# A graph attention kernel in which SyncE fetches, one by one, a part of the node rows that GpSimd gathered

## The chip, the cores and the metric

The kernel runs on one core of one Trainium2 chip. The metric is the device time of one execution, in microseconds (us). The kernel before takes 4064.29 us, the median of three runs (4062.84 to 4064.88). An engine is named as in the profile: PE (TensorE, matrix products), DVE (VectorE, elementwise work), ACT (ScalarE), POOL (GpSimd) and SP (SyncE, which here only issues transfers). A queue that carries a q, as SPq, is the engine's own issuing of transfers.

## The reference

A graph has 6250 nodes of 256 numbers and 200000 edges, sorted by destination; every edge has 32 numbers of its own. The nodes pass a layer norm and two graph attention layers (four heads, then one). What matters of a layer, with the self loops and the edge gate left out:

```python
hx = (x @ Wg).reshape(n, h, f)
al = leaky_relu(dot(hx, a_s)[src] + dot(hx, a_d)[dst] + dot(he, a_e), 0.2)
m = segment_max(al, dst)
al = exp(al - m[dst])
al = al / segment_sum(al, dst)[dst]
out = segment_sum(hx[src] * al[:, :, None], dst) + b
```

So for every edge the row of its source node is fetched (`hx[src]`), weighted, and summed over the edges of one destination. The sources are in no order: the fetch is a gather of 200000 rows, in each of two layers.

## The kernel before

The 200000 edges are cut into 1563 chunks of 128, and these into 66 superchunks of 24 chunks (the last two are shorter). A node table in DRAM, `T[0]` or `T[1]`, holds for each node its 256 transformed numbers and a few logit terms, 268 or 260 numbers of four bytes that an edge needs. `steps` lists the 66 superchunks of the first layer and then the 66 of the second; the loop in `edges` makes one of them per pass, and prepares the next one (`nx`) in the same pass.

The parts of a pass, in the order of the code:

- `nodes` (L936, L938): SP loads the rows of 112 destination nodes of the superchunk two ahead into `tw`. The row number is a register that SP loads first from `base_i` (L927). Each of four `tw` buffers comes free when `finish` of the superchunk four back has read it.
- `load_lb`, `load_ea`, `load_fl` (L896, L921): SP loads the position rows `lb` (384 KB) and the edge numbers `ea` (768 KB) of two superchunks together, every second pass, and flags `fl` every fourth.
- `gather(nx)` (L871): POOL issues 24 indirect transfers, one per chunk, the last chunk first. Each fetches 128 rows of the table into one column of `G`. There are three buffers of `G`.
- `logits(st)` (L1071 and on), `ends`, `links`, `maxima`: DVE makes the logits and the running maxima, with small transposes on PE. This needs all 24 columns of `G`.
- `spread`, `parts`, `rphase1`, `rphase2`, `adst`: the edge part of `nx`. `parts` reads `tw` on DVE (L1021, for two superchunks at a time in every second pass), PE multiplies `ea` (L968), ACT takes the result (L969), PE collects it in `zad`.
- `scale(st)` (L1180): DVE multiplies all 24 columns of `G` by the weights. `carried` adds the sums brought over from the superchunk before.
- `sums(st)` (L1192): PE sums the rows by destination, 24 products with a one-hot matrix `S`.
- `rows3` (L1326 in the first layer, L1331 in the second): SP stores finished node rows.
- `edge_rows(nx)` (L1057, L1060): DVE turns `zad` into rows `rt` and sums them to `ade`, which `logits` of the next pass reads.
- `onehots(nx)` (L1008): DVE makes `S` of the next superchunk.
- `finish(pv)` (L1208 to L1279): DVE and ACT close the superchunk before. `evict(st)` (L1197): ACT takes the sums out of PSUM. `rows1`: PE and ACT turn the closed rows.

Every engine works through its own instructions in the order of the code and waits by semaphores for what it reads or overwrites. Nothing reorders them. The transfers that SP issues take turns on eight completion semaphores (DMAHW0 to DMAHW7): before SP issues one, the transfer eight back must have landed. The last three superchunks of a layer have their own code (`ending`).

Of the kernel before, what the change touches and what calls it, by code (L numbers as in the profile page):

```python
# [22 lines left out]
F32 = mybir.dt.float32  # L23
BF = mybir.dt.bfloat16
I32 = mybir.dt.int32
AF = mybir.ActivationFunctionType
# [5 lines left out]
P = 128  # L32
C = 24
# [13 lines left out]
def cuts(E):  # L47

    n = -(-E // P)
    k = -(-n // C)  # L50
    if k == 1:
        return [n]
    rest = n - C * (k - 2)
    return [C] * (k - 2) + [rest - rest // 2, rest // 2]


class Layer:

    def __init__(self, l):
        self.l = l
        self.H = H = HEADS[l]
        self.F = D // H
        self.p = D
        self.g = D + H
        self.one = D + H + 1
        self.gr = self.ad = D + H + 2
        self.m = self.ln = D + 2 * H + 2
        self.W = D + 3 * H + 2  # L70
        self.MW = D + 2 * H + 2
        self.TW = self.MW + (2 if l == 0 else 0)
# [7 lines left out]
class Kernel:  # L80
    def __init__(self, nc, tc, a, N, E, ctx):
        self.nc, self.tc, self.a, self.N, self.E, self.ctx = nc, tc, a, N, E, ctx
        self.cs = cuts(E)
        self.NS = len(self.cs)
        self.NCH = sum(self.cs)
        self.L = [Layer(0), Layer(1)]

    def pool(self, name, bufs=1, ctx=None, **kw):
# [548 lines left out]
    def edges(self, ctx):  # L637
        nc = self.nc
        self.gp += [self.pool(f"gath{i}", 1, ctx) for i in range(1, 3)]
        self.sp = self.pool("onehot", 2, ctx)  # L640
        self.wp = self.pool("work", 2, ctx)
        self.np_ = self.pool("nodes", 2, ctx)
        self.xp = self.pool("index", 1, ctx)
        self.ps_y = self.pool("ps_y", 1, ctx, space=PSUM)
        self.ps_1 = self.pool("ps_1", 1, ctx, space=PSUM)
        self.ps_f = self.pool("ps_f", 1, ctx, space=PSUM)
        self.lf = self.ps_1.tile([P, 512], F32, name="lf")
        nc.vector.memset(self.lf[0:4, 0:1], -BIG)
        steps = self.steps
        self.state = {0: None, 1: None}  # L650
        self.nodes(steps[0])
        self.gather(steps[0])
        if self.NS % 2:
            self.load_lb(1)
        self.spread(steps[0])
        self.parts(steps[0])
        self.blocks(steps[0])
        drain(self.rphase1(steps[0]))
        self.load_ea(1)
        self.rphase2(steps[0])  # L660
        self.adst(steps[0])
        self.onehots(steps[0])
        drain(self.soon)
        self.edge_rows(steps[0])

        pv = late = None
        self.ahead, self.rest = 1, None
        for k, st in enumerate(steps):
            nx = steps[k + 1] if k + 1 < len(steps) else None
            if st["s"] + 2 >= self.NS:  # L670
                continue
            for q in steps[k + 1:k + 3]:
                if q["L"] is st["L"] and "tw" not in q:
                    self.nodes(q)
            self.load_lb(k + 2)
            left = 99
            if self.ahead < len(self.groups):
                left = self.groups[self.ahead][0] - 2 - (self.ahead + 2 >= len(self.groups)) - k
            if self.rest is None and left <= 2:
                gi = self.index_load(self.ahead, self.xp)  # L680
                self.rest = self.index_group(self.ahead, self.xp, gi)
            if st["s"] + 3 == self.NS:
                self.ending(st, *steps[k + 1:k + 3], pv, late, steps[k + 3] if k + 3 < len(steps) else None)
                pv = late = None
                continue
            self.gather(nx)
            drain(self.logits(st))
            self.ends(st)
            self.spread(nx)
            self.parts(nx)  # L690
            y = self.rphase1(nx)
            next(y)
            self.links(st)
            if late:
                self.rows2(late)
            self.load_fl(k + 1)
            self.blocks(nx)
            drain(self.maxima(st))
            drain(y)
            self.load_ea(k + 2)  # L700
            self.rphase2(nx)
            self.adst(nx)
            if "S" not in st:
                self.onehots(st)
            drain(self.scale(st))
            self.carried(st)
            self.sums(st)
            if late:
                self.rows3(late)
                late = None  # L710
            self.edge_rows(nx)
            self.onehots(nx)
            if pv:
                drain(self.finish(pv))
            self.evict(st)
            if pv:
                self.rows1(pv)
                late = pv
            self.index_on(left)
            if st["s"] + 4 == self.NS:  # L720
                drain(self.finish(st))
            if k >= 6:
                next(self.late, None)
                next(self.late, None)
            pv = st
        self.flag()

# [126 lines left out]
    def flag(self):  # L854
# [6 lines left out]
        nc.vector.tensor_reduce(f[:, 0:1], ps[0:1, 0:n], axis=AX.X, op=OP.add)  # L861
        nc.vector.tensor_scalar(self.flag_i, f[:, 0:1], 0.0, None, op0=OP.is_equal)

    def gather(self, st):
        nc, L = self.nc, st["L"]
        st["G"] = G = self.G0 if st["k"] == 0 else self.gp[st["k"] % 3].tile([P, C, 270], F32, name="G")
        n = self.N
        idx = self.src[:, st["o"]:st["o"] + st["C"]]
        last = st["C"] - 1
        for c in (range(0) if st["k"] == 0 and self.CX > last else (last, *range(last))):  # L870
            nc.gpsimd.indirect_dma_start(  # L871
                out=G[:, c, 0:L.TW], out_offset=None, in_=self.rows[L.l][0:n * (1 + L.l), :],
                in_offset=bass.IndirectOffsetOnAxis(ap=idx[:, c:c + 1], axis=0))
# [582 lines left out]
def drain(g):  # L1456
    for _ in g:
        pass
# [22 lines left out]
def layout(inputs):  # L1481
# [3 lines left out]
    cs = cuts(E)  # L1485
    NS, NCH = len(cs), sum(cs)
    a = {"x": np.concatenate([x, np.zeros((2 * P, D), np.float32)])}
# [7 lines left out]
    nx = np.full(EP, END_DST, np.int32)  # L1495
# [3 lines left out]
    srcp, dstp, dnxp = (np.empty((P, NCH), np.int32) for _ in range(3))  # L1499
# [5 lines left out]
    for s, c in enumerate(cs):  # L1505
        e0, e1 = o * P, (o + c) * P
        nx[e1 - 1] = END_DST
        for t, v in ((srcp, sp), (dstp, dp), (dnxp, nx)):
# [11 lines left out]
        o += c  # L1520
    a.update(gsrc=sp.reshape(-1, 1), gdst=gdst.reshape(-1, 1), gdrow=gdst,
             gea=np.ascontiguousarray(eap.T))
    a.update(src=srcp, dst=dstp, dnx=dnxp, drow=drow, prow=prow, sdst=sdst,
             dpv=np.ascontiguousarray(prow[:, 3].T),
             srow=np.ascontiguousarray(sp[:cs[0] * P].reshape(P, -1).T),
# [26 lines left out]
```

## Time and profile before

| what | value |
|---|---|
| median of three runs | 4064.29 us |
| the profiled execution's own time | 4068.59 us |
| its span (first to last instruction) | 4066.2 us |
| busy: POOL, DVE, PE, ACT | 3012.7, 2855.0, 2696.3, 519.9 us |
| indirect transfers of L871 | 3102, 2959.9 us busy, 954 ns each |
| granted clock of TensorE | 0.789 |

The profile counts an engine as busy while it runs an instruction of its own; issuing a transfer counts as busy on POOL, where the engine makes the descriptors, but not on SP. A row of the groups has the line, engine and operation, what is written and read, the count, the busy time with the mean of one, and the idle time before them with what ended most of it. A row of the waits has the waiting engine, line and tile, what ended the wait, and then us in total, times, longest. A row of the timeline has the start and duration in us.

### The profile page before, as it was taken

How to read it: one execution, taken by the hardware profiler on the slowest of the kernel's cores; microseconds unless marked ns; L12 is line 12 of the kernel's file. 1: busy time of each engine (PE TensorE's matmuls, PEld its weight loads, DVE VectorE, ACT ScalarE, POOL GpSimd, SP SyncE). 2: the span in 40 equal slices, each digit the busy share in tenths (PEclk: the TensorE clock that was granted, in tenths of full speed). 3: DMA queues.
4: the chain of work that ended last, by engine and by line, in shares of the span. 5: the costliest groups of instructions: out<-in, count | busy, mean ns of one | idle time of the engine just before them, and what ended most of it. 6: DMA issues, size and time to landing. Idle time of an engine off the chain costs nothing.

```text
span 4066.2 us, 34155 instructions
## 1 busy us (share of the span) xinstructions
PE 2696.3 (66%) x9878; PEld 1737.4 (43%) x9878; DVE 2855.0 (70%) x6188; ACT 519.9 (13%) x1158; POOL 3012.7 (74%) x3255
## 2 busy tenths in 40 slices
PE   8776666666666766766646656666657666666665
PEld 6454444444444444444433433433434334334334
DVE  7887877877877877777856656656566566565666
ACT  5211111111111111111110000000000000000000
POOL 5777777777777777777747777777777777777775
PEclk9888888887887788888777787777777777777777
DMA  7455555555555555555434455455455445445443
GB/s 251 137 152 140 146 149 140 145 149 144 142 150 147 140 148 147 141 147 148 134 103 133 136 142 141 130 141 140 132 140 140 134 137 143 132 137 142 132 137 96
DMA packets 231085, 576.17 MB, mean 142 GB/s; under 512 B 63097, under 2 KB 87871, under 8 KB 230825
## 3 DMA queue, kind: packets, MB, share of 16 engines
q0 software_dynamic: 150144, 422.75, 39.6%
q1 hardware_dynamic: 80331, 150.52, 11.4%
q8 instruction: 79, 1.29, 0.1%
q14 instruction: 115, 0.94, 0.1%
q10 hardware_dynamic: 416, 0.67, 0.1%
HBM read 542.72 MB, written 31.09 MB: 141 GB/s over the span
## 4 chain that ended last, share of the span: by engine, by line
POOL 53%; issue 19%; DVE 19%; DMA 4%; PE 4%; ACT 1%; SPq 0%; DVEq 0%; ACTq 0%; POOLq 0%
POOL G L871 53%; DVE G L1180 6%; DMA G<-T,src 4%; DVE S L1008 3%; DVE lb L992 1%; PE ps L444 1%; PE y L968 1%; PE u L1192 1%; DVE rt L1057 1%; DVE m L1131 1%; DVE ade L1060 0%; DVE G L1169 0%; DVE fb L1126 0%; DVE al L1075 0%; DVE al L1073 0%
## 5 line engine op out<-in xcount | busy, mean ns | idle before, releaser
L871 POOL DMA_INDIRECT G<-T,src x3102 | 2959.9, 954 | 1001.1 <-issue 929.7
L1192 PE MATMUL u<-G,S 128*128 128x270 f32 (+1 forms) x6252 | 1617.9, 423 | 250.8 <-DVE G L1170 247.2
L1192 PEld LDWEIGHTS u<-G,S 128*128 128x128 f32 x6252 | 1295.4, 209 | 585.6 <-DVE G L1170 314.7
L1180 DVE TENSOR_TENSOR G<-G,kps 128x6144 f32<-128x6144 f32 (+2 forms) x140 | 853.3, 6099 | 0.0
L1071 DVE TENSOR_TENSOR G<-rt,G 128x96 f32<-128x96 f32 (+1 forms) x132 | 30.3, 229 | 910.3 <-DMA G<-T,src 910.0
L1099 PE MATMUL lf<-ident,fb 128*36 128x128 f32 (+1 forms) x132 | 49.5, 375 | 710.8 <-DVE fb L1088 684.3
L1008 DVE TENSOR_TENSOR S<-kps,loc 128x3072 f32<-128x3072 f32 x132 | 437.5, 3315 | 4.6
L968 PE MATMUL y<-ea,webd 64*128 64x256 f32 (+1 forms) x1056 | 396.7, 846 | 51.4 <-ACT R L969 51.4
L977 PE MATMUL zad<-R,wea 128*64 128x384 f32 (+1 forms) x1056 | 301.2, 711 | 158.4 <-ACT R L969 158.1
L969 ACT ACTIVATE R<-y,webd 128x1024 f32<-128x1024 f32 (+2 forms) x264 | 235.6, 892 | 1226.0 <-PE y L968 741.5
L1099 PEld LDWEIGHTS lf<-ident,fb 128*36 128x36 f32 (+1 forms) x132 | 15.6, 118 | 752.5 <-DVE fb L1088 725.2
L977 PEld LDWEIGHTS zad<-R,wea 128*64 128x64 f32 x1056 | 86.7, 185 | 426.0 <-ACT R L969 340.6
L968 PEld LDWEIGHTS y<-ea,webd 64*128 64x128 f32 x1056 | 125.6, 291 | 125.5 <-ACT R L969 70.4
L1197 ACT ACTIVATE U<-u 128x270 f32<-128x270 f32 (+1 forms) x132 | 51.9, 394 | 645.9 <-PE u L1192 645.9
L1029 PE MATMUL zad<-a,Q 128*128 128x12 bf16 (+1 forms) x132 | 26.1, 198 | 160.1 <-DVE a L1024 160.1
L444 PE MATMUL fin<-wg,h1T 128*128 128x260 f32 x264 | 128.7, 638 | 3.7 <-ACT h1T L1287 3.7
L1057 DVE STREAM_TRANSPOSE rt<-zad 128x768 f32<-128x768 f32 (+1 forms) x130 | 124.5, 957 | 5.1 <-PE zad L1043 5.1
L992 DVE TENSOR_TENSOR lb<-lb,kps 128x1536 bf16<-128x1536 bf16 (+1 forms) x68 | 113.5, 1670 | 0.0
L1222 ACT ACTIVATE mw<-mw,mg 128x2 f32<-128x2 f32 x66 | 19.7, 298 | 623.9 <-DVE mg L1221 623.9
L1029 PEld LDWEIGHTS <-Q 128*128 128x128 bf16 x132 | 16.0, 121 | 172.7 <-DVE a L1024 165.8
L1043 PE MATMUL zad<-lb,aq 128*128 128x384 bf16 (+1 forms) x264 | 86.5, 421 | 0.0
L444 PE MATMUL ps<-wg,hT 128*128 128x266 f32 x292 | 83.2, 410 | 1.7 <-ACT hT L326 1.6
(190 smaller groups left out, 2109.8 us busy)
## 6 DMA issues: line engine op xcount, KB each, us to landing
G<-T,src POOLq DMA_INDIRECT x3102, 2.8
ea<-in_ea_dram SPq DMA_DIRECT2D x64, 768.0 KB
lb<-locrow SPq DMA_DIRECT2D x64, 384.0 KB
T<-t1row SPq DMA_DIRECT2D x66, 227.5 KB
tw<-T SPq DMA_DIRECT2D x66, 225.8 KB
tw<-T SPq DMA_DIRECT2D x66, 117.2 KB
tw<-in_x_dram SPq DMA_DIRECT2D x66, 112.0 KB
out_dram<-fb SPq DMA_DIRECT2D x64, 112.0 KB
```

What stands on the lines that cost most here:

```text
L444: self.nc.tensor.matmul(ps[:, :L.MW], hT[:, k, :], self.wg[L.l][:, k, :], start=(k == 0), stop=(k == 1))
L871: nc.gpsimd.indirect_dma_start(out=G[:, c, 0:L.TW], out_offset=None, in_=self.rows[L.l][0:n * (1 + L.l), :], in_offset=bass.IndirectOffset ...
L968: nc.tensor.matmul(y[:, i, :n], self.webd[l][r, :], ea[r, w], start=True, stop=True)
L969: nc.scalar.activation(R[:, :, w], y[:, :, :n], AF.Relu, bias=self.be[l])
L977: nc.tensor.matmul(st["zad"][i * PH:(i + 1) * PH, o], self.wea[l][0], R[:, i, w], start=True, stop=False)
L992: V.tensor_tensor(lb[:, :, :n], lb[:, :, :n], self.k_part.unsqueeze(2).to_broadcast([P, i, n]), op=OP.is_equal)
L1008: nc.vector.tensor_tensor(st["S"][:, c0:c1, :], self.k_iota.unsqueeze(1).to_broadcast(w), self.loc[:, o + c0:o + c1].unsqueeze(2).to_broad ...
L1043: self.nc.tensor.matmul(st["zad"][:, o], st["aq"].rearrange("p k j -> p (k j)"), st["lb"][:, w], start=False, stop=True)
L1057: V.transpose(rv[:, :32 * c].rearrange("p (b n) -> p b n", b=2), z.rearrange("p (b n) -> p b n", b=2)[:, :, :16 * c])
L1099: self.nc.tensor.transpose(self.lf[0:e.shape[1], 1:P + 1], e, self.ident)
L1180: nc.vector.tensor_tensor(v, v, pw[:, c0:c1, :].unsqueeze(3) .to_broadcast([P, c1 - c0, H, L.F]), op=OP.mult)
L1192: nc.tensor.matmul(st["u"][:, :L.W], S[:, i, :], G[:, i, 0:L.W], start=(j == 0), stop=(j == c - 1))
```

## The change

`sides` names every third superchunk of a layer, 3, 6, 9 and so on to 60: 20 in each layer. For these POOL leaves out the gather of the last chunk. Its 128 rows are fetched by SP instead, each with a transfer of its own. A list of the 128 source numbers is loaded into a row `si`; eight loads bring 16 of them each into SP's registers; each register gives the place of one row in the table, and the row goes to one partition of a buffer `side`, of which there is one. `side` is a generator that hands out one transfer at a time, and `pump` draws 14, 15 and 14 of them at three places in a pass, over the three passes before the superchunk is worked on (43 x 3 = 129, the list and 128 rows). `placed(nx)`, at the end of the third pass, has ACT copy `side` into the last column of `G`.

In every pass `edge_rows(nx)` moves from its place ahead of `onehots(nx)` to the end of the pass, and in one pass of each layer the additional `finish(st)` comes after it.

The core of the diff:

```diff
+def sides(cs):
+    return [s for s in range(3, len(cs) - 3, 3)]
@@ edges
+        self.fp = self.pool("rows", 1, ctx)
+        self.flow = iter(())
         for k, st in enumerate(steps):
             nx = steps[k + 1] if k + 1 < len(steps) else None
+            if k + 3 < len(steps) and st["L"] is steps[k + 3]["L"] and steps[k + 3]["s"] in self.sides:
+                self.flow = self.side(steps[k + 3])
             if st["s"] + 2 >= self.NS:
                 continue
+            self.pump(14)
             for q in steps[k + 1:k + 3]:
                 if q["L"] is st["L"] and "tw" not in q:
                     self.nodes(q)
@@
                 self.rows2(late)
+            self.pump(15)
             self.load_fl(k + 1)
@@
             self.load_ea(k + 2)
+            self.pump(14)
             self.rphase2(nx)
@@
-            self.edge_rows(nx)
             self.onehots(nx)
@@
-            if st["s"] + 4 == self.NS:
-                drain(self.finish(st))
             if k >= 6:
                 next(self.late, None)
                 next(self.late, None)
+            self.placed(nx)
+            self.edge_rows(nx)
+            if st["s"] + 4 == self.NS:
+                drain(self.finish(st))
@@
+    def pump(self, n):
+        for _ in range(n):
+            if next(self.flow, self) is self:
+                break
+
+    def side(self, st):
+        nc, L, j = self.nc, st["L"], self.sides.index(st["s"])
+        idx = self.fp.tile([1, P], I32, name="si")
+        nc.sync.dma_start(idx, self.a["side"][j:j + 1, :])
+        st["row"] = R = self.fp.tile([P, self.L[0].TW], F32, name="side")[:, 0:L.TW]
+        yield
+        for b in range(0, P, 16):
+            _, rows = nc.values_load_multi_w_load_instructions(
+                idx[0:1, b:b + 16], engines=(mybir.EngineType.SP,), min_val=0, max_val=self.N - 1,
+                skip_runtime_bounds_check_because="sources are nodes")
+            for i, r in enumerate(rows):
+                nc.sync.dma_start(R[b + i:b + i + 1, :], self.T[L.l][ds(r, 1), 0:L.TW])
+                yield
+
+    def placed(self, st):
+        if "row" in st:
+            drain(self.flow)
+            L = st["L"]
+            self.nc.scalar.activation(st["G"][:, st["C"] - 1, 0:L.TW], st["row"], AF.Copy)
@@ gather
         for c in (range(0) if st["k"] == 0 and self.CX > last else (last, *range(last))):
+            if c == last and "row" in st:
+                continue
             nc.gpsimd.indirect_dma_start(
@@ layout
+    last = [sum(cs[:s + 1]) - 1 for s in sides(cs)] or [0]
+    a.update(side=np.ascontiguousarray(srcp[:, last].T))
```

How the rows of SP stand now is seen in the first layer, at a place where one side buffer is full and the next begins. Before, SP's rows from one store of finished node rows (`T_61<-t1row`) to the next were these, where `tw_175` is the buffer of destination rows, ISA the register arithmetic of the transfer behind it, and TENSOR_LOAD the load of a register:

```order
L1326 DMA T_61<-t1row_171 112x520
L927 TENSOR_LOAD base_i
L936 ISA
L936 DMA tw_175<-T_60 112x268
L938 ISA
L938 DMA tw_175<-in_x_dram 112x256
L921 DMA fl<-flags 4x516 x2
L1326 ISA
L1326 DMA T_61<-t1row_173 112x520
```

In the changed kernel the last row of one side buffer, the store, and the first rows of the next side buffer follow each other:

```order
L895 DMA side<-T_60 1x268
L1369 ISA
L1369 DMA T_61<-t1row_171 112x520
L887 DMA si<-in_side_dram 1x128
L891 TENSOR_LOAD si
L895 ISA
L895 DMA side<-T_60 1x268
```

Thirteen rows of `side` now stand between that store and the load of `tw_175`, which followed the store directly.

On DVE, in the first layer, `edge_rows` (`rt`, `ade`) stood before the one-hot matrix `S` and the closing of the superchunk before (`cnt`, then more):

```order
L448 TENSOR_TENSOR t1row_173<-fin,bias_373 128x260
L1057 STREAM_TRANSPOSE rt<-zad 128x768
L1060 TENSOR_REDUCE ade<-rt 128x96
L1005 COPY kps<-lastloc 128x1
L1008 TENSOR_TENSOR S<-kps,loc 128x3072
L1208 TENSOR_SCALAR cnt<-U 128x1
```

In the changed kernel they stand behind the last rows of that closing and directly ahead of the next superchunk's logits (`G<-rt,G`):

```order
L1312 TENSOR_TENSOR fb<-fa,fb 128x256
L1320 TENSOR_TENSOR t1row_171<-tw_175,hw 128x256
L1322 TENSOR_TENSOR t1row_171<-t1row_171,fb 128x256
L1100 STREAM_TRANSPOSE rt<-zad 128x768
L1103 TENSOR_REDUCE ade<-rt 128x96
L1114 TENSOR_TENSOR G<-rt,G 128x24x4
```

The two rows moved past `S` and the closing of a superchunk; nothing else on DVE moved.

1 line of the change is left out of this document (added).

## The prediction

> **What bounds the kernel now.** I read the page first, then the waits in total and by layer, POOL's gathers by stretch, and SP's timeline over two passes. The waits of the whole run (us in total, times, longest):
>
> ```profile
> POOL G L871 <- issue: 929.7, 3050, 0.3
> DVE G L1071 <- DMA G<-T,src: 910.0, 123, 20.4
> POOL G L871 <- DMA T<-t1row: 40.5, 1, 40.5
> ```
>
> 3050 of POOL's 3102 gathers waited for nothing but the 0.3 us that lies between any two of them; DVE waited 910 us for gathers. The gathers alone, in a stretch of each layer (length, busy time and count):
>
> ```profile
> 200.00:1940.00 1740.00, 1319.61 (x1379) 0.83 0.53 146
> 2150.00:3980.00 1830.00, 1386.06 (x1457) 0.75 0.50 138
> ```
>
> 1740 / 1379 = 1.262 us and 1830 / 1457 = 1.256 us for one gather, against 954 ns busy: POOL issues gathers back to back through both layers. A pass is 24 of them, 30.2 us, and a gather left out is worth 1.26 us as long as nothing else becomes longer than POOL. What DVE has to spare is the wait for gathers in these two stretches (the first layer, then the second):
>
> ```profile
> DVE G L1071 <- DMA G<-T,src: 257.0, 54, 9.4
> ...
> DVE G L1071 <- DMA G<-T,src: 601.6, 61, 11.3
> ```
>
> That is 4.8 us in a pass of the first layer and 9.9 us in one of the second. So the question is SP. Its transfers over two passes, and two that follow each other without a wait:
>
> ```profile
> 1012.95 0.41 SPq L896 DMA_DIRECT2D ea<-in_ea_dram  x1
> 1019.26 0.34 SPq L1326 DMA_DIRECT2D T<-t1row  x1
> 1026.83 0.33 SPq L936 DMA_DIRECT2D tw<-T  x1
> 1028.19 0.32 SPq L938 DMA_DIRECT2D tw<-in_x_dram  x1
> 1038.07 0.60 SPq L921 DMA_DIRECT2D fl<-flags  x2
> 1049.08 0.33 SPq L1326 DMA_DIRECT2D T<-t1row  x1
> 1056.62 0.33 SPq L936 DMA_DIRECT2D tw<-T  x1
> 1057.97 0.34 SPq L938 DMA_DIRECT2D tw<-in_x_dram  x1
> 1058.36 0.61 SPq L896 DMA_DIRECT2D lb<-locrow  x1
> ...
> 91.94 0.32 SPq L936 DMA_DIRECT2D tw<-T  x1
> 92.45 0.32 SPq L938 DMA_DIRECT2D tw<-in_x_dram  x1
> ```
>
> SP is nearly empty: some ten transfers in 60 us.
>
> **The change, part by part.** *The gather left out*: 20 superchunks in each of two layers, 40 x 1.26 = 50.4 us off POOL, all on the path.
>
> *SP's rows.* What one row costs is bounded by these durations (minimum/median/maximum in ns):
>
> ```profile
> L936 SPq FUSED_REGOPS  x132: 37/37/56, 85.2 to 3983.4; - x132
> L936 SPq MOVE tw<-T x132: 29/29/43, 88.0 to 3983.6; - x132
> L936 SPq DMA_DIRECT2D tw<-T x132: 317/328/360, 88.1 to 3994.3; - x132
> L921 SPq DMA_DIRECT2D fl<-flags x68: 248/292/635, 70.8 to 4009.3; - x68
> L927 SPq TENSOR_LOAD <-base_i x196: 261/282/546, 84.6 to 4013.7; - x196
> ```
>
> A transfer with a row number from a register has the same three instructions as L936. From start to start that took 92.45 - 91.94 = 0.51 us, of which 0.32 us was the transfer over 112 partitions; the one over 4 partitions takes 0.25 us at its least. One partition is nearest to that: 0.51 - 0.32 + 0.25 = 0.44 us, with 0.51 us as the other end. Eight completion semaphores allow eight rows under way; a gather, which moves 128 rows of the same table, lands in 2.8 us:
>
> ```profile
> G<-T,src POOLq DMA_INDIRECT x3102, 2.8
> ```
>
> 2.8 / 8 = 0.35 us is under 0.44, so landing does not hold the rows up.
>
> *The eight loads of 16 registers* are not in the trace; L927 loads one. The low end is one trip for all, 0.28 us; the high end 16 trips, 16 x 0.282 = 4.5 us. I take one trip and 15 more register writes at the price of a MOVE, 0.28 + 15 x 0.029 = 0.72 us, since register writes are the only row of that kind. This is the least certain number here.
>
> *SP's sum over two passes*, of 2 x 30.2 - 0.8 = 59.5 us: 86 rows x 0.44 = 37.8; 5.3 loads x 0.72 = 3.8; its own ten transfers, durations 3.6 with 0.2 us of register work each and two loads, 5.3. Then what holds the eight semaphores: after `lb` at 1058.36 all transfers together stay busy until about 1068 (third number from the right, the share of the engines):
>
> ```profile
> 1062.00:1066.00 4.00, 0.79 (x5) 0.42 (x3) 0.00 (x0) 0.84 (x3) 2.94 (x4) 1.00 0.81 182
> 1066.00:1068.00 2.00, 0.00 (x0) 0.00 (x0) 0.86 (x3) 0.00 (x0) 1.70 (x2) 0.99 0.59 181
> 1068.00:1070.00 2.00, 0.97 (x6) 0.65 (x6) 1.47 (x7) 0.00 (x0) 1.39 (x3) 0.50 0.31 92
> ```
>
> (The share is 0.81, 0.59, then 0.31.) So `lb` may hold its semaphore for 9.6 us; seven more transfers go out in 0.6 + 7 x 0.44 = 3.7, and SP stands still for up to 5.9. The list `si` must land before its first load, 2.8 us every third pass, 1.9 in two. Together 54.7 us of 59.5: it fits, with 4.8 to spare.
>
> *Whom the rows hold up.* The waits of SP's queue before:
>
> ```profile
> SPq L936 <- DVE fb L1307: 1040.5, 62, 43.5
> SPq L896 <- PE y L968: 975.3, 65, 35.9
> SPq L1326 <- ACT t1row L1297: 658.4, 65, 19.7
> ```
>
> SP spent its time waiting to be allowed to load `tw`, `ea` and to store. Fourteen rows (6.2 us and a load) after the store at 1019.26 end at 1026.5, ahead of the 1026.83 at which `tw` was allowed to go; fifteen more end at 1036; so the rows fill waits that were there. The exception is the first row of each side buffer. It overwrites the one buffer, so it waits for ACT's copy, which waits for the gathers of that superchunk, that is until about when DVE starts its logits; `tw` stands behind thirteen rows, and lands some 0.6 + 5.7 + 1.0 + 2.8 = 10 us after that start. Its reader:
>
> ```profile
> 1032.37 0.26 DVE L1071 TENSOR_TENSOR G<-rt,G 128x96 f32<-128x96 f32 x1 [3.63 <-DMA G<-T,src]
> ...
> 1036.25 0.37 DVE L1021 CAST a<-tw 128x8 bf16<-128x8 f32 x1
> ```
>
> reads 3.9 us after the start, in every second pass. So in 20 of the 40 cases DVE stands for about 6 us. DVE's spare time over the six passes between such cases, 29 us or more, takes it, and POOL has a whole `G` buffer of lead; I cost it at nothing. If SP falls behind for another reason this cover is gone.
>
> *ACT's copy.* Nearest row, 128x256 between the same memories:
>
> ```profile
> L1253 ACT ACTIVATE hw<-tw x66: 583/585/600, 169.3 to 2063.0; 128x256 f32<-128x256 f32 x66
> ```
>
> 0.6 us, behind the landing of the last gather and ahead of DVE's logits: 40 x 0.6 to 1.0 us out of DVE's spare time, nothing on POOL. *`edge_rows` later*: the same 1.35 us of DVE, closer to the wait for the gathers; `tw` is set free 1.35 us sooner. Nothing either way. *The first pass*: `tw` of superchunks 1 and 2 now stands behind the first thirteen rows; 0 to 3 us, taken as 0.
>
> Sum: 50.4 us off. The profiled execution has a span of 4066.2 and a time of 4068.59 us, 0.1% over the median 4064.29; the difference is taken off the median, 4013.9 us, rounded to 4014.
>
> **The rivals.** *Each register is a trip of its own* (slower). A load of 16 then takes up to 4.5 us; per two passes 5.3 x (4.5 - 0.72) = 20.0 us more, 15.2 over what fits. Rows are drawn in 60 passes of each layer, 60 pairs in all: 60 x 15.2 = 912 us, 4926 us. SP would be the bound, `tw` and the rows late, POOL waiting for `G`. It decides from 0.72 + 4.8 / 5.3 = 1.6 us for a load. For it speaks that one register takes 282 ns where a MOVE takes 29, so a trip is what costs; against it, only that 16 numbers lie side by side in one row. The Trainium skill, page "Runtime: NRT & Kernel Launch", section "Instruction fetch mechanics", states that such a load costs about 200 ns per register even in bulk. By that figure, an estimate, a load takes 3.2 us and the kernel 4014 + 60 x (5.3 x 2.48 - 4.8) = 4515 us; the single load here, 282 ns, agrees with it, and no run here shows the bulk.
>
> *A row costs as much as a `tw` transfer*, 0.51 us: 86 x 0.07 = 6.0, 1.2 over per pair, 72 us given back: 4086 us. For it: it is the only transfer with a register's row number that the trace has; against it, the 0.25 us over 4 partitions.
>
> *Nothing comes of it*: the gather is saved but another engine holds the pass at 30.2 us: 4064 us. The 4.8 us that DVE waits in each pass speak against it.
>
> **How the numbers follow.** A load as taken, all fits: 0.42, 4006 to 4022 us (three us of the first pass above, and 8 us, 0.2%, about what a measurement of this kernel tells from no change). Register by register: 0.40, from 4022 up to 4926 us. A dear row: 0.12, 4014 to 4150 with stalls beside it. Nothing: 0.06. The likeliest is the first, 4014 us. Cases of both signs hold much, so the range goes from 4006 to 4700: 4700 is a load of 0.72 + (686 / 60 + 4.8) / 5.3 = 3.8 us, and what lies above it I hold for 0.13. Faster by over 0.2%: 0.42 and a hundredth of the dear row, 0.43. Within: 0.06 and another, 0.07. Slower: 0.40 and 0.10, 0.50.
>
> **What would show it.** Right: 3062 gathers, still 1.26 us apart; 40 copies on ACT of 0.6 us; TENSOR_LOAD of `si` under 1.6 us; rows 0.44 us apart; DVE's wait at L1021 some 100 us in all, and its wait for gathers or the copy still some us in a pass. Wrong: loads of some us; POOL with waits on PE or DVE at its first gather of a superchunk; ACT's copy waiting for SP's rows rather than for gathers; DVE waiting for `tw` in every second pass.

## The result and the profile after

The changed kernel takes 4063.64 us, the median of 12 runs (4058.86 to 4072.08), against 4064.14 us for the kernel before in the same comparison (12 runs, 4059.49 to 4066.95). The ratio is 1.0002, with a 95% interval of 0.9994 to 1.0010: no change, where 50 us were forecast off. The profiled execution after has a span of 4067.4 us.

The waits of the whole run after answer to the first rows shown of before (us in total, times, longest):

```profile
POOL G L914 <- issue: 912.2, 2981, 3.6
POOL G L914 <- DMA T<-t1row: 56.5, 1, 56.5
POOL G L914 <- PE fin L1328: 40.1, 12, 6.7
...
DVE G L1114 <- DMA G<-T,src: 572.4, 70, 20.4
DVE a L1064 <- DMA tw<-T: 291.2, 53, 12.1
DVE G L1114 <- ACT G L903: 51.8, 16, 4.3
```

L914 is the gather, L1114 DVE's logits, L1064 DVE's first reading of `tw`, L903 ACT's copy. Two things are new. DVE waits 291 us for `tw`, for which it waited about 3 us before; and POOL waits 12 times, up to 6.7 us, for PE, all in the first layer, where it had issued its gathers back to back. (What it waits for are PE's sums: the first gather of superchunk 34, for example, starts at 1098.2 us, 0.3 us after the end of the sums of superchunk 31, which read the same one of the three `G` buffers. The row names a later PE instruction, which ended closest to it.) In the first layer DVE hardly waits for gathers any more, but for `tw`. Its first waits from 200 to 1940 us, where those for gathers were 257.0 us before:

```profile
DVE a L1064 <- DMA tw<-T: 213.1, 29, 12.1
DVE G L1114 <- ACT G L903: 48.6, 15, 4.3
...
DVE G L1114 <- DMA G<-T,src: 15.5, 4, 4.4
```

Where this happens is seen from two rows of DVE's last steps of a superchunk, of before and then of after (duration in ns, minimum/median/maximum; first and last start in us). The first row of each pair is the closing in the first layer, the second in the second layer:

```profile
L1277 DVE TENSOR_TENSOR t1row<-tw,hw x66: 410/418/420, 171.7 to 2066.1; 128x256 f32<-128x256 f32 x66
L1307 DVE SCALAR_TENSOR_TENSOR fb<-tw,mw,fb x66: 467/485/486, 2156.6 to 4054.3; 128x256 f32<-128x256 f32 x66
```

```profile
L1320 DVE TENSOR_TENSOR t1row<-tw,hw x66: 411/418/422, 176.7 to 2098.3; 128x256 f32<-128x256 f32 x66
L1350 DVE SCALAR_TENSOR_TENSOR fb<-tw,mw,fb x66: 465/485/486, 2187.0 to 4059.5; 128x256 f32<-128x256 f32 x66
```

The last superchunk of the first layer is closed at 2098.3 us against 2066.1, 32.2 us later; from there to the last one of the second layer it takes 1961.2 us against 1988.2, 27.0 us less. The second layer has the gain, the first has a loss of about that size. The first layer was to save 20 gathers, 25.2 us, and lost 32.2, so it misses 57.4 us. POOL's waits account for nearly all of it: the 12 waits for PE are 40.1 us, and its wait at the change of layers grew by 16.0 us, from 40.5 to 56.5. The same division is used for every run below: "first layer" is the last start of the first row, "second layer" the distance from there to the last start of the second.

The gathers by stretch after, as shown of before, agree:

```profile
200.00:1940.00 1740.00, 1288.85 (x1348) 0.82 0.52 144
2150.00:3980.00 1830.00, 1385.80 (x1458) 0.76 0.51 139
```

In the second layer POOL still issues one gather in 1830 / 1458 = 1.255 us. In the first it issued 1348 in the stretch, against 1379 before, one in 1.291 us.

SP's queue after, in the first layer (200 to 1940 us):

```profile
SPq L895 <- DMA lb<-locrow: 133.0, 28, 6.6
SPq L895 <- ACT pen L1002: 113.6, 18, 11.4
SPq L891 <- DMA si<-in_side_dram: 36.7, 19, 2.3
SPq L895 <- DMA ea<-in_ea_dram: 25.1, 20, 3.1
SPq L1369 <- ACT t1row L1340: 3.1, 6, 0.9
```

L895 is a row's transfer, L891 a load of 16 registers, L1369 the store. The second line is the wait of a side buffer's first row for ACT's copy of the buffer before: L1002 is ACT's instruction directly behind the copy, and 18 of the 19 side buffers of this stretch wait. SP's waits to be allowed to load or store, which were 1561 us in this stretch before (597 at the store, 411 at `ea`, 377 and 46 at the two loads of `tw`, 130 at `fl`), are gone but for a few us: the store waits 3.1 us in all. An SP that no longer waits for anybody's permission, and that others wait for, is late itself. Its transfers around such a first row:

```profile
1019.99 0.34 SPq L1369 DMA_DIRECT2D T<-t1row  x1
1020.42 0.23 SPq L887 DMA_DIRECT2D si<-in_side_dram  x1
1032.04 5.55 SPq L895 DMA_DIRECT2D side<-T  x13
1038.42 0.32 SPq L979 DMA_DIRECT2D tw<-T  x1
```

and ACT's instructions there:

```profile
1030.69 0.40 ACT L1240 ACTIVATE U<-u 128x270 f32<-128x270 f32 x1 [3.08 <-PE u L1235]
1030.98 0.38 ACT L1330 ACTIVATE h1T<-fin 128x256 f32<-128x256 f32 x1
1031.59 0.43 ACT L903 ACTIVATE G<-side 128x268 f32<-128x268 f32 x1 [0.23 <-issue]
```

After `si` at 1020.42, SP stands until ACT's copy (L903) has freed the buffer at 1032.0; `tw` goes behind thirteen rows. The copy itself waited for neither gathers nor rows: it follows ACT's instruction before it by 0.23 us, and that stands behind ACT taking the sums of the pass out of PSUM (L1240), for which ACT waited 3.08 us. In all 40 cases the copy starts at most 0.5 us after the end of ACT's work before it.

SP's own prices, in the view of one line:

```profile
L891 SPq TENSOR_LOAD <-si x320: 1132/1232/1408, 114.6 to 3897.9; - x160
L895 SPq DMA_DIRECT2D side<-T x5120: 224/228/937, 116.0 to 3906.2; - x197
```

The period of a side buffer, that is of three passes, is the distance from one `si` to the next. After, in the first layer (19 of them):

```profile
L887 SPq DMA_DIRECT2D si<-in_side_dram x19: 231/238/244, 199.9 to 1855.5; - x19
```

(1855.5 - 199.9) / 18 = 92.0 us. GpSimd's 71 gathers of 1.26 us would take 89.5, and its 72 of before 90.7. So SP's period is longer than either. In the second layer it is not:

```profile
L887 SPq DMA_DIRECT2D si<-in_side_dram x19: 268/273/281, 2213.0 to 3826.0; - x19
```

(3826.0 - 2213.0) / 18 = 89.6 us, about what 71 gathers take.

### The profile page after: what moved, and what is told of

The parts are those of the page before. It is cut to its first block, busy times and chain, and to the rows that moved or that the text cites. A ratio compares the mean times of both kernels' runs of the same rounds, so it can differ in the third digit from the quotient of the medians.

```text
span 4067.4 us, 50369 instructions
## 1 busy us (share of the span) xinstructions
PE 2625.4 (65%) x9878; PEld 1710.9 (42%) x9878; DVE 2851.9 (70%) x6188; ACT 537.3 (13%) x1198; POOL 2970.8 (73%) x3215
## 5 line engine op out<-in xcount | busy, mean ns | idle before, releaser
L914 POOL DMA_INDIRECT G<-T,src x3062 | 2918.6, 953 | 1049.6 <-issue 912.2
L1114 DVE TENSOR_TENSOR G<-rt,G 128x96 f32<-128x96 f32 (+1 forms) x132 | 30.3, 230 | 624.3 <-DMA G<-T,src 572.4
L1011 PE MATMUL y<-ea,webd 64*128 64x256 f32 (+1 forms) x1056 | 361.4, 775 | 42.6 <-ACT R L1012 42.6
L1064 DVE CAST a<-tw 128x8 bf16<-128x8 f32 (+3 forms) x68 | 13.5, 198 | 291.2 <-DMA tw<-T 291.2
L1011 PEld LDWEIGHTS y<-ea,webd 64*128 64x128 f32 x1056 | 114.2, 265 | 107.7 <-ACT R L1012 61.6
L1240 ACT ACTIVATE U<-u 128x270 f32<-128x270 f32 (+1 forms) x132 | 51.9, 394 | 795.2 <-PE u L1235 778.6
L450 PE MATMUL fin<-wg,h1T 128*128 128x260 f32 x264 | 116.1, 583 | 3.8 <-ACT h1T L1330 3.8
L1035 DVE TENSOR_TENSOR lb<-lb,kps 128x1536 bf16<-128x1536 bf16 (+1 forms) x68 | 113.6, 1671 | 0.0
L1152 DVE TENSOR_TENSOR_SCAN cl<-fl,cl,lf 4x129 f32<-4x129 f32 (+1 forms) x130 | 60.9, 468 | 39.6 <-PE zad L1072 36.0
```

The source lines that it names most:

```text
L450: self.nc.tensor.matmul(ps[:, :L.MW], hT[:, k, :], self.wg[L.l][:, k, :], start=(k == 0), stop=(k == 1))
L914: nc.gpsimd.indirect_dma_start(out=G[:, c, 0:L.TW], out_offset=None, in_=self.rows[L.l][0:n * (1 + L.l), :], in_offset=bass.IndirectOffset ...
L1011: nc.tensor.matmul(y[:, i, :n], self.webd[l][r, :], ea[r, w], start=True, stop=True)
L1035: V.tensor_tensor(lb[:, :, :n], lb[:, :, :n], self.k_part.unsqueeze(2).to_broadcast([P, i, n]), op=OP.is_equal)
L1152: V.tensor_tensor_scan(cl[:H, :], fl[:H, :], lf[:H, 0:P + 1], init, op0=OP.add, op1=OP.max)
```

## The experiments

The times below are medians; the ratio to the kernel before, run beside each, has its 95% interval. The theory formed from the profile after was that SyncE's time per three passes, the wait for the copy in it, is what the first layer now waits for; the rivals were the copy on ACT, the traffic of the rows, the moved edge rows, and later the place of `tw` in SP's queue.

| kernel | time, us | ratio | first layer, us later than 2066.1 | second layer, us against 1988.2 |
|---|---|---|---|---|
| changed kernel | 4063.64 | 1.0002 [0.9994, 1.0010] | +32.2 | -27.0 |
| rows at constant places | 4006.16 | 0.9857 [0.9842, 0.9872] | -32.4 | -25.9 |
| two side buffers | 4007.63 | 0.9864 [0.9848, 0.9879] | -32.3 | -25.7 |
| edge rows only | 4056.97 | 0.9982 [0.9973, 0.9991] | -7.4 | -3.7 |
| second layer only | 4029.13 | 0.9915 [0.9902, 0.9929] | -14.8 | -27.3 |
| first layer only | 4093.43 | 1.0064 [1.0044, 1.0083] | +34.4 | -3.3 |
| loads of four | 4277.63 | 1.0522 [1.0506, 1.0538] | +138.5 | +74.7 |
| edge rows back | 4075.20 | 1.0025 [1.0016, 1.0034] | +34.9 | -28.2 |
| `lb` on ACT's queue | 4297.29 | 1.0581 [1.0564, 1.0598] | +139.0 | +90.0 |
| one index buffer | 4069.40 | 1.0015 [1.0006, 1.0025] | +32.5 | -26.3 |
| two side buffers, edge rows back | 4010.95 | 0.9875 [0.9858, 0.9891] | -25.6 | -29.8 |
| `tw` first | 4008.09 | 0.9864 [0.9848, 0.9881] | -30.7 | -23.7 |
| `tw` first, once more | 4007.39 | 0.9858 [0.9841, 0.9874] | -29.5 | -24.0 |
| `tw` first, loads of four | 4162.19 | 1.0249 [1.0231, 1.0267] | +69.5 | +25.1 |
| two side buffers and `tw` first | 4009.10 | 0.9863 [0.9846, 0.9879] | -29.8 | -24.3 |

Line numbers in the rows are those of the changed kernel unless said otherwise.

### Rows at constant places

```diff
-            _, rows = nc.values_load_multi_w_load_instructions(
-                idx[0:1, b:b + 16], engines=(mybir.EngineType.SP,), min_val=0, max_val=self.N - 1, ...)
+            rows = range(b, b + 16)
-                nc.sync.dma_start(R[b + i:b + i + 1, :], self.T[L.l][ds(r, 1), 0:L.TW])
+                nc.sync.dma_start(R[b + i:b + i + 1, :], self.T[L.l][r:r + 1, 0:L.TW])
```

> The changed kernel with the 128 rows of a side buffer taken from the fixed places 0 to 127 of the table: no loads of registers and no register work ahead of a row, so SP spends less per row (some 0.27 instead of 0.42 us) and none of the 9.9 us of loads per buffer. It leaves out that the rows are those of the sources, so the values are not the reference's. If SP's own work paces the first layer: both layers gain, about 4014 us (4010 to 4022). If the copy on ACT, the rows' traffic or the late edge_rows cost the time: about 4064 us, as the changed kernel.

It took 4006 us, some 4 us under the 4010 to 4022 expected; the 7 us that the moved edge rows give by themselves (below) were not known then. The same number of rows moves, and the copy and the moved edge rows are there; what is gone is the eight loads and the register work of every row. SP's queue in the first layer (200 to 1950 us; here L893 is the row, L1367 the store, L1000 what was L1002):

```profile
SPq L893 <- ACT pen L1000: 226.2, 19, 13.6
SPq L1367 <- ACT t1row L1338: 201.7, 31, 20.3
```

The first row of a side buffer now stands for the copy twice as long as in the changed kernel, 226 us against 114, with `tw` behind it just the same; and nothing is lost. SP comes early and has time: its waits for the permission to store are back, 202 us. So neither the number of rows, nor the copy on ACT, nor the wait at the first row as such costs the gain. (Here the rows lie side by side in the table; that scattered rows do not cost it either is shown by the next experiment.)

### Two side buffers

```diff
-        st["row"] = R = self.fp.tile([P, self.L[0].TW], F32, name="side")[:, 0:L.TW]
+        st["row"] = R = self.fp.tile([P, self.L[0].TW], F32, name="side", bufs=2)[:, 0:L.TW]
-        di = pool.tile([P, 2, 4 * C], I32, name="gi", bufs=2)
+        di = pool.tile([P, 2, 4 * C], I32, name="gi", bufs=1 if pool is getattr(self, "xp", None) else 2)
```

(The second line makes room for the first.)

> Two side buffers, so that the first row of one does not wait for ACT's copy of the one before (114 us of SP in the first layer of the changed kernel, 88 us in the second). To make room one index buffer of two goes. If SP paces the first layer: it needs some 2 us less per pass there, more than the 0.7 us per pass that it is over, and only the loss of the first passes stays: about 4025 us (4015 to 4035). If the copy or edge_rows on DVE's path cost the time: 4064 us, since the copy stays where it is.

It took 4008 us, with the scattered rows, the loads and the register work in place. That is under the 4015 to 4035 us expected: the loss at the start of the layer was made up later. DVE's waits of the whole run:

```profile
DVE G L1114 <- DMA G<-T,src: 767.0, 97, 20.2
DVE a L1064 <- DMA tw<-T: 49.3, 15, 7.9
DVE G L1114 <- ACT G L903: 45.6, 12, 5.5
```

The wait for `tw` falls from 291 to 49 us, and DVE waits for gathers again. SP's queue in the first layer (200 to 1940 us) has no wait for the copy left, and waits for the permission to store once more:

```profile
SPq L895 <- DMA lb<-locrow: 149.9, 28, 6.7
SPq L1369 <- ACT t1row L1340: 52.2, 18, 22.0
SPq L891 <- DMA si<-in_side_dram: 35.4, 19, 2.3
```

The period of a side buffer is 87.9 us there. Taking 113.6 us of standing, some 6 us per side buffer, out of SP's time was enough. The control with the index buffer's line alone,

> The changed kernel with one side buffer as it is, and only the index buffer cut from two to one, which is the other half of the edit in the version with two side buffers. Theory (the second side buffer made the gain, by taking away the wait for ScalarE's copy): no change, 4064 us (4055 to 4072). Rival (the gain of that version came from the index buffer): 4008 us.

took 4069 us, so that line costs some 5 us if anything, and the side buffer made the gain.

### One layer at a time, and the edge rows

```diff
-            if k + 3 < len(steps) and st["L"] is steps[k + 3]["L"] and steps[k + 3]["s"] in self.sides:
+            if st["L"].l == 1 and k + 3 < len(steps) and st["L"] is steps[k + 3]["L"] and steps[k + 3]["s"] in self.sides:
```

> The changed kernel with SP's rows in the second layer alone; edge_rows late in both. If SP's load in the first layer is what costs: the first layer is as before and the second gains 20 gathers of 1.26 us, 25 us: about 4039 us. If the late edge_rows costs in the first layer: about 4064 us or more.

and the same with `st["L"].l == 0`:

> Rows fetched by SyncE in the first layer only; the second layer gathers all chunks as before. Theory (first layer paced by SyncE, second layer all gain): the first layer's loss stays, 32 us at the first logits of the second layer, and the second layer has only the later edge rows' 4 us: 4064 + 32 - 4 = 4092 us (4080 to 4100). Rival (the loss is in the change of layers or in the second layer): 20 gathers of 1.26 us less and 7 us for the edge rows, 4064 - 25 - 7 = 4032 us.

4029 and 4093 us (4039 and 4092 had been expected). The table shows the two halves apart: rows in the first layer alone cost it 34 us and leave the second at the edge rows' 3 us; rows in the second layer alone give it 27 us. Not explained is that in the kernel with rows in the second layer alone the first layer, where only the edge rows are moved, was 14.8 us shorter, twice the 7.4 that they give by themselves (below); its profiled execution was the fastest of five, 5 us under their median.

The kernel before, with the edge rows turned at the end of the pass and nothing else:

```diff
-            self.edge_rows(nx)
             self.onehots(nx)
...
+            self.edge_rows(nx)
+            if st["s"] + 4 == self.NS:
+                drain(self.finish(st))
```

> The kernel before with edge_rows moved to the end of the pass and nothing else. If SP paces: no difference, 4064 us (within 8). If the late edge_rows lengthens DVE's pass in the first layer, where DVE has least to spare: up to 30 us slower, 4094 us.

It gained 7 us, which nothing in the prediction gave. The gathers of a stretch in each layer, of before and then of this kernel:

```profile
400.00:1900.00 1500.00, 1137.57 (x1190) 0.82 0.53 145
2200.00:3950.00 1750.00, 1325.41 (x1393) 0.75 0.50 138
```

```profile
400.00:1900.00 1500.00, 1136.02 (x1196) 0.82 0.54 146
2200.00:3950.00 1750.00, 1324.79 (x1397) 0.75 0.51 138
```

Six more gathers fit into the first stretch and four into the second, so they follow each other 6 and 4 ns closer (1500 / 1190 against 1500 / 1196 us, and likewise), on a count that is good to about 1 ns. The gathers themselves became shorter by that: 1137.57 / 1190 = 956 ns busy against 1136.02 / 1196 = 950, and 951 against 948 in the second layer. Over 3102 gathers that is some 15 us, of the right sign and order for the 7 to 11 us seen. Why a gather is shorter when DVE turns the edge rows at another time was not tried. Put back in the changed kernel,

> The edge rows are turned at their old place again; the side buffers stay as in the changed kernel. Theory (the first layer goes at SyncE's pace, only the second at GpSimd's): the 7 us that the later edge rows gave by themselves come back as a loss only in the second layer, some 3 to 4 us: 4067 us (4062 to 4072). Rival (the later edge rows, behind the copy, are what costs the changed kernel its gain): 4015 us.

the time was 4075 us, 8 more than expected; in the profiles the first layer is 3 us later than in the changed kernel and the second 1 us shorter, so the rest of it isn't placed. The period of a side buffer in the first layer is 92.0 us, as in the changed kernel: the place of the edge rows does not set it. Put back in the version with two side buffers,

> Two side buffers, with the edge rows turned at their old place. Theory (the gain is made of two terms that add: 40 gathers of 1.26 us, 50 us, and 7 us for the edge rows, as they gave by themselves): 4064 - 50 = 4014 us (4009 to 4020). Rival one (the later edge rows are needed, since the copy stands ahead of them): 4025 us or more. Rival two (they do nothing once SyncE is free of the copy): 4007 us.

it was 4011 us, 53 less than the kernel before beside it: the 40 gathers of 1.26 us are 50.4 of these. The first layer misses the edge rows (-25.6 against -32.3 us), while the second gives 4 us back (-29.8 against -25.7), which isn't explained.

### Loads of four registers

```diff
-        for b in range(0, P, 16):
+        for b in range(0, P, 4):
-                idx[0:1, b:b + 16], engines=(mybir.EngineType.SP,), min_val=0, max_val=self.N - 1,
+                idx[0:1, b:b + 4], engines=(mybir.EngineType.SP,), min_val=0, max_val=self.N - 1,
```

> The row numbers are brought into registers four at a time in place of sixteen, so SyncE has 32 loads per side buffer in place of 8. From the profile after, one load of 16 is 1.23 us and a load of one is 0.28 us, so a load of four should be 0.47 us and 32 of them 15.1 us in place of 9.9 us: some 5.3 us more of SyncE's time per side buffer, nothing else moved. Theory (SyncE paces the first layer, has slack in the second): 20 x 5.3 = 106 us longer, about 4170 us (4120 to 4200), with the first layer's logits late by that amount. Rival one (ScalarE's copy comes late for VectorE, SyncE is not the bound): no change, 4064 us. Rival two (the transfers' traffic slows the gathers): no change either, since the rows are the same.

It took 4278 us, twice the expected loss. A load of four was dearer than reckoned (0.47 us):

```profile
L891 SPq TENSOR_LOAD <-si x1280: 298/558/797, 115.0 to 4132.5; - x183
```

32 x 0.558 - 8 x 1.232 = 8.0 us per side buffer in place of 5.3. The first layer came out 106.3 us later than in the changed kernel, 5.3 of the 8.0 per side buffer (the first row's wait for the copy shrank, from 113.6 to 71.3 us in this layer, as SP came later to it), and the second, which had been thought to have room, 101.7. DVE waited 753 us for `tw`. The direction and the engine were right; that the second layer is far from SP's limit was wrong.

### `lb` on ACT's queue

```diff
-            self.nc.sync.dma_start(dst(tile[:, i:i + n]), src)
+            (self.nc.scalar if name == "lb" else self.nc.sync).dma_start(dst(tile[:, i:i + n]), src)
```

> The one large transfer lb (once per two superchunks) is issued on ScalarE's queue in place of SyncE's. In the profile after, SyncE's rows stand 297 us behind lb in 60 waits, 133 us of it in 28 waits of the first layer. Theory (SyncE's total of work and waits per two superchunks is over POOL's time there, by about 1 to 2 us after a start that loses 25): taking 4 to 5 us per pair out lets the first layer run at GpSimd's pace again, 4015 us (4005 to 4035). Rival one (only the wait of a side buffer's first row for ScalarE's copy matters, whatever else SyncE does): it stays, 4055 to 4064 us. Rival two (the transfer makes ScalarE wait for lb's buffer, and ScalarE's order is tight): slower, 4075 us or more, with waits of ScalarE's queue at that line.

It was to free SP of `lb`, and took 4297 us. SP's rows stand behind `lb` all the more, 579 us where it was 297:

```profile
SPq L895 <- DMA lb<-locrow: 578.8, 55, 24.2
SPq L895 <- ACT G L903: 161.7, 19, 11.3
```

The timeline of SP, and the one transfer of ACT's queue in the same 22 us:

```profile
1011.96 0.34 SPq L1369 DMA_DIRECT2D T<-t1row  x1
1012.50 19.27 SPq L895 DMA_DIRECT2D side<-T  x14
1032.61 0.32 SPq L979 DMA_DIRECT2D tw<-T  x1
```

```profile
1022.40 0.51 ACTq L939 DMA_DIRECT2D lb<-locrow  x1
```

The fourteen rows take 19.3 us, where thirteen take 5.2 without a wait (a row below); in the trace SP issues none of them between 1018.3 and 1031.1. The transfers of both queues take turns on the same eight completion semaphores. The next row's turn is on the semaphore that `lb` takes, so SP waits first for ACT to come to `lb` in its own order, at 1022.4, and then for 384 KB to land. Moving a transfer to another engine did not take it out of SP's line. The theory's number did not come of it, since SP's standing grew where it was to shrink. The time lies where the second rival had it (4075 us or more), but not by that mechanism: ACT never stood more than 0.2 us ahead of `lb`.

### `tw` first

```diff
-            self.pump(14)
             for q in steps[k + 1:k + 3]:
                 if q["L"] is st["L"] and "tw" not in q:
                     self.nodes(q)
             self.load_lb(k + 2)
+            self.pump(14)
```

> One side buffer; SyncE issues a pass's tw and lb ahead of the first 14 rows in place of behind them, nothing else. The first row still waits for ScalarE's copy, but tw no longer stands behind that wait. Theory one (SyncE's total, its work plus that wait, paces the first layer, wherever the wait stands): little changes in the sum, 4050 to 4070 us, and the lateness moves to the edge features, the rows and their copy, so that VectorE waits at its logits for the copy (over 150 us against 52) in place of at tw. Rival (only the place of tw behind the wait costs): VectorE's wait for tw goes from 291 us to under 60, and the time to 4007 to 4015 us.

Here the theory as it was put fell: 4008 us, with one side buffer, as the rival had it. DVE's waits for `tw` went to 37 us. But SP's queue in the first layer (200 to 1950 us) shows that the wait did not only change its place:

```profile
SPq L895 <- DMA lb<-locrow: 99.2, 19, 7.4
SPq L891 <- DMA si<-in_side_dram: 87.7, 19, 8.0
...
SPq L895 <- ACT pen L1002: 5.6, 4, 2.0
```

The wait for the copy, 113.6 us, is 5.6; together with the landing of `si` it was 150 us and is 93. SP issues `tw` and `lb` where it would have stood, `si` lands behind `lb`, and by then the copy is mostly done. The period of a side buffer:

```profile
L887 SPq DMA_DIRECT2D si<-in_side_dram x19: 256/281/353, 200.4 to 1789.7; - x19
```

(1789.7 - 200.4) / 18 = 88.3 us, 3.7 less than in the changed kernel and just under the 89.5 of GpSimd, as with the constant rows (88.3) and the two side buffers (87.9). So the result could still come from the sum. To tell the place of `tw` from SP's sum, SP was given 8.0 us more per side buffer with `tw` still first:

> tw and lb ahead of the first 14 rows, as in the version at 4008 us, and the row numbers brought in by four: 32 loads of 0.558 us in place of 8 of 1.232 us, 8.0 us more of SyncE's time per side buffer; nothing else. Theory (SyncE's time per three superchunks decides, and putting tw first helped only because it shortened SyncE's standing by some 5 us per side buffer): SyncE has some 4.3 us of waits on permissions left per side buffer of the first layer, so 8.0 - 4.3 = 3.7 us per side buffer come through, times 20 = 74 us in the first layer and up to as much in the second: 4080 us or more (4060 to 4200), with VectorE's waits for tw above 300 us. Rival (it was the place of tw behind the wait, SyncE has time): no change from 4008 us, VectorE's waits for tw below 80 us.

It took 4162 us, and the version with `tw` first beside it 4007 us:

> The version with tw and lb ahead of the first 14 rows once more, on the chip of the two others, so that the step to loads of four is read on one chip: 4008 us again (4004 to 4013), 0.986 of the kernel before.

DVE's waits of the whole run with `tw` first and loads of four, and then the period:

```profile
DVE a L1064 <- DMA tw<-T: 478.8, 39, 21.3
DVE G L1114 <- ACT G L903: 263.3, 31, 18.2
```

```profile
L887 SPq DMA_DIRECT2D si<-in_side_dram x19: 274/275/353, 204.6 to 1899.0; - x19
```

(1899.0 - 204.6) / 18 = 94.1 us. With `tw` ahead of the row that waits, 5.8 us more per side buffer make `tw` late again and cost 155 us. With the constant rows above, `tw` stood behind 226 us of waits and nothing was lost. So moving `tw` is neither needed nor enough: SP's time per three passes, with its standing, against GpSimd's 89.5 us is what decides. How much of the standing would hurt if `tw` did not stand behind it was not taken apart further.

### Both cures

The lines of "two side buffers" and of "`tw` first" together:

> Two side buffers and tw first, together. Theory (either cure alone brings the first layer back to GpSimd's pace, and then the gathers bound it): no more than either, 4007 us (4003 to 4011), VectorE's waits for gathers near 765 us as in each. Rival (what VectorE still waits for tw and for the copy, some 40 to 95 us in each, is on the path): 3970 to 3995 us.

4009 us, no more than either. DVE waits 805 us for gathers there, so the gathers bound it again. Either cure alone beats both kernels by 1.4%; `tw` first needs no memory.

An earlier run of this kernel (6200 us), and two of "`tw` first, loads of four" (6361 and 6478 us), fell on chips on which the kernel before itself took 4688 and 4746 us. There some of SP's register moves, which take 29 ns otherwise, took up to 1.45 us in the trace, and the granted clock of TensorE was 0.74 for the kernel before in place of 0.79. What ailed these chips isn't known, and nothing is concluded from these runs.

## Why the prediction was wrong

**The bound and the gain of a gather: right.** 3062 gathers, 1.255 us apart in the second layer. Where SP keeps up, 40 gathers less are worth the 50 us: 53 in the version with two side buffers and the edge rows in their old place.

**The row: right, a little dear.** 0.44 us was taken. Thirteen rows that follow each other without a wait:

```profile
1124.13 5.22 SPq L895 DMA_DIRECT2D side<-T  x13
```

(5.22 - 0.23) / 12 = 0.416 us. The rival of a dear row (0.51) is out. A smaller slip is in DVE's spare time in the first layer: 4.8 us is the mean of its 54 waits for gathers; over the 58 passes of that stretch it is 257.0 / 58 = 4.4 us.

**The load of 16 registers: mis-sized.** 0.72 us was taken, with 0.28 and 4.5 as ends; it is 1.23. The row by which it was sized did not stay: one register, the load of `base_i`, took 0.282 us in the kernel before, and takes 0.537 in the changed one, among the rows:

```profile
L970 SPq TENSOR_LOAD <-base_i x196: 273/537/705, 83.6 to 4018.7; - x196
```

Why it does isn't known. Four take 0.558 us (above) and sixteen 1.232, so from four to sixteen a further register costs 56 ns, twice a MOVE and far from a trip. The Trainium skill, page "Runtime: NRT & Kernel Launch", section "Instruction fetch mechanics", has about 200 ns per register even in bulk. The page speaks of loads out of HBM, while `si` is a tile on the chip, and for that the trace does not agree: 1232 / 16 = 77 ns. (The 282 ns of a single load, which the prediction took for agreement, are 40% over the page's figure too.) The rival of a trip each, which gave 4926 us (4515 by the page), is out: 1.23 is under the 1.6 us from which it was to decide. But the load used 2.7 of the 4.8 us that were to spare.

**SP's sum: the step that failed.** The prediction had 54.7 us per two passes, 82.1 per three, of 89.3. Per three passes, against what the changed kernel's first layer shows:

| item, per side buffer | predicted, us | measured, us | from |
|---|---|---|---|
| 128 rows | 56.7 | 53.2 | 0.416 each |
| 8 loads | 5.7 | 9.9 | 1.232 each |
| standing behind `lb` and `ea` | 8.9 | 8.4 | (133.0 + 25.1) / 18.9 |
| landing of `si` | 2.8 | 1.9 | 36.7 / 18.9 |
| first row's wait for the copy | 0 | 6.0 | 113.6 / 18.9 |
| SP's own transfers and the rest | 8.0 | 12.6 | what is left of 92.0 |
| sum | 82.1 | 92.0 | period of `si` |

(The waits are those of 1740 us, which are 1740 / 92.0 = 18.9 periods.) The largest missing term is the wait of the first row for ACT's copy. The prediction had seen it ("The exception is the first row of each side buffer") and priced it for DVE only: `tw` late by 6 us in 20 cases, "I cost it at nothing". It is SP's time too, and there it was left out. With the loads mis-sized by 4.2 us and the last item by 4.6 (0.8 of it the three loads of `base_i`), the 7 us to spare became 2.5 too many. Without the wait 86.0 us are left, under GpSimd's 89.5, and that is what the second side buffer showed. Without the error of the loads the sum would have fitted as well, though by 1.7 us; the constant rows, which lack the loads and the register work of each row, showed that side.

The prediction also had the copy wait for gathers. In the trace it waits only for its place in ACT's order, behind the sums of the pass. So a pass that is late because of `tw` makes the copy late, and with it SP: the 6.0 us are no fixed price, but in part the effect of SP's own lateness.

**The cover named for it was the right one to doubt.** "If SP falls behind for another reason this cover is gone": DVE's wait was not the 6 us in every second pair, but, in the first layer alone (200 to 1940 us), 213 us in 29 waits, one at every reading in that stretch, since SP was late throughout.

**The rest.** ACT's copy was 0.42 us and not 0.6, and cost little. DVE waits at its logits 52 us for it. The edge rows, "Nothing either way", gave 7 us. The first pass, taken as 0, was not: in the trace the logits of superchunk 6 start at 302.0 us against 277.0 before, 25 us later. So most of the 32 us are lost by then, and what the longer period does is that the layer neither makes this up nor gains its 25 us. With two side buffers the logits of superchunk 6 are 19 us late, and the layer still ends 32 us early. Before, these first passes took 25 us each, less than the 30.2 on which the prediction's sum rests, so SP had still less room there; that this is the reason was not tried.

**The rivals.** The time came out at that of "nothing comes of it", but not by its way: no engine held the passes at 30.2 us. The first layer went to SP's pace and lost 32 us, the second gained 27, and that the two cancel is chance. The mark given for a wrong forecast, POOL waiting for PE, DVE for `tw`, is what the profile after shows.

## What to carry to other kernels

When an engine is given work that fills its waits, add up its whole time per period, its standing included: a wait that costs the readers of its data nothing still takes up the time of the queue in which it stands. A single buffer that is refilled as soon as it is read puts the reader's lateness into the loader's sum; a second buffer, or other transfers issued in that wait, takes it out again. The price of an instruction, too, can change with what its engine does around it: the load of one register went from 0.28 to 0.54 us. And look, in each stage apart, which engine sets the period after the change: here two layers with opposite signs made a zero.

## What the runs showed of the hardware

- SP loads sixteen registers from one row in 1.23 us, four in 0.56 and one in 0.54 when it issues single rows in between; in the kernel before, without these, one took 0.28.
- A transfer of one row with its place in a register takes SP 0.23 us of issue and 0.41 to 0.42 from start to start, with a 37 ns register operation and a 29 ns MOVE beside it.
- Transfers of SP and of ACT take turns on the same eight completion semaphores in this program: a 384 KB load issued by ACT held SP's rows for 12.8 us, 4.1 of them before ACT issued it.
- The gathers became shorter by 3 to 6 ns and came 4 to 6 ns closer to each other when DVE turned the edge rows at the end of the pass. The cause is open.
